# A two-layer vision kernel on one core: V loads one step ahead, score matmuls of two units in one block, and six small changes of order

## The chip, the cores and the metric

The kernel runs on one core of a Trainium2 chip. Times are microseconds on the device, from the start of the program to its end. Engines are named as in the profile: PE is TensorE (the matrix engine; PEld is its loading of weights), DVE is VectorE, ACT is ScalarE, POOL is GpSimd, and SP is SyncE, whose queue issues all the transfers (DMAs) of this kernel in program order. SBUF is the on-chip memory, PSUM the eight banks that PE writes and the other engines read.

## The reference, cut to what matters

The input `x` is 2 images of 56 x 56 tokens with 384 channels, all in float32. Two layers follow each other.

```python
# layer 0
def layer0(x):
    qkv = layer_norm(x) @ w_qkv + b_qkv          # 12 heads of 32; q is scaled by 32 ** -0.5
    # each query sees the 7 x 7 keys around it (the window is moved inside at the borders)
    scores = einsum('bnhwd,bnhwkd->bnhwk', q, k_nb) + bias   # bias by relative position, per head
    attn = softmax(scores)
    x = x + einsum('bnhwk,bnhwkd->bnhwd', attn, v_nb) @ w_proj + b_proj
    return x + gelu(layer_norm(x) @ w1 + b1) @ w2 + b2       # hidden width 1536

# layer 1
def layer1(x):
    p = layer_norm(x) @ w_in + b_in              # inner width 768
    local = depthwise_conv_3x3(p)
    lr, rl = ema(local, axis=W), ema(local, axis=W, reverse=True)    # y = 0.6 * y_before + 0.4 * x
    tb, bt = ema(local, axis=H), ema(local, axis=H, reverse=True)
    mixed = layer_norm(0.25 * (lr + rl + tb + bt) + local)
    x = x + mixed @ w_out + b_out
    return x + gelu(layer_norm(x) @ w1 + b1) @ w2 + b2
```

## The kernel before, in words

The order of the instructions is written out by hand; the framework only adds the waits that data, buffers and banks ask for. Each engine runs its own instructions in program order, so an instruction that waits holds everything behind it on its engine.

**Attention, 0 to about 725 us.** The work is cut into 14 groups (`n`) of 8 image rows, a group into 4 windows (`j`) of 8 x 14 = 112 queries (`TT`), and a window into 3 units (`hg`) of 4 heads each. That makes 56 windows and 168 units. The loop over `s` (L692) has one step for each unit and four more. The keys that a window's queries see are cut into two chunks, in the middle rows and inner columns into three, of 100 to 120 keys (`m` is the number of chunks): 108 units have two chunks and 60 have three. Ahead of the loop stands a startup (L632–676) that normalises the first groups and makes their queries, keys and values.

In step `s`, PE makes the scores of unit `s` (`scores`, L508: per chunk four matmuls, one for each head, on 32 rows of the array each). They are written to two tiles `sc[0]` and `sc[1]`, two heads in each and one bank per head. Then it applies the values of unit `s - 2` (`values`, L544) and sums the numerators with a matrix of ones (L550), and then takes one piece of full-size work, if one is left: queries or keys of a later group (L385), values of a later group (L423), or a projected tile of the output (L569); in some steps also transposes of normalised input (L356). In the same step DVE takes what PE made in the step before (for instance L577, the projected tile plus the residual `xr`), then adds the bias to the scores in two halves (`biased`, L521), then adds up the chunks of unit `s - 1` (`gathered`, L534). ACT makes the exponentials (L528) and evicts the queries, keys and values (L395, L410, L430).

When a window's three units are done, its output is copied (`take`, L477), and its sums of exponentials are transposed (`gather`, L481) and put by POOL into a column of `history` (L482). A step later `invert` makes the reciprocals (L486) and POOL spreads them (`wide`, L488). A step after that `divide` transposes them back (L492) and multiplies (L494). At the end of the stage two operations over `history` and a minimum (L803–809) decide whether all sums were in a safe range; if not, attention is made again by a slow path, which does not run here.

A window's values are loaded from DRAM into a tile `vt` (L464), one transfer for each chunk, when the `Window` object is made, which is in the step of its own first unit; `vt` has two buffers. The other transfers of a step are issued before it, in this order: stores (`store_all`, L629), residuals (`load_residual`, L558, three buffers `xr`, each free when its store has landed), bias tables (L315, 1344 KB), and in the last windows the parts of the MLP's weights (L612, 768 KB each).

**MLP 1 and the way in, about 725 to 1725 us.** The tokens go in groups of up to four tiles of 128 (`groups`). Per group PE makes 12 hidden tiles (`hidden`, L1035; evicted with GELU by ACT, L1044), then the output rows (`tokens`, L1051; added and measured by DVE in the loop at L1379), and the input projection of layer 1 (`project_in`). Beside it, DVE makes the convolution and the running means of layer 1, image by image: `Band` for the 3 x 3 convolution and the scans along rows, `Columns` for the scans along columns. These are cut into small steps, and `beside.go(us)` lets as many of them into the program as fit the given time, at each place where it is called. `Columns` first turns its input around: `turn` (L1171–1180) makes four copies of 128 x 392 on ACT. `turn` is called from three places: from `steps` if nothing was turned before (the first unit of work of each image), again inside the first half, and by the unit of work ahead of it. The result goes to DRAM (`mix_d`).

**The way out and MLP 2, about 1725 us to the end.** Here a group's mixed tiles are loaded (`load_mix`), measured (`measure`, L1238: PE transposes them, DVE takes the statistics), projected (`project_out`, L1252–1261, on PE L1051 with `w_out`, added by DVE at L1258), and the second MLP follows. `measure_beside` (L1244) puts a tile's measurement behind every second hidden tile of the group before; `half_way` is the first group that holds tokens of the second image, whose mixed tiles are the last to be finished.

Layer norms are made by `Norm`: statistics on DVE (L214, L215), `close` (L219 on DVE, then a power on POOL, L222), `shift` (L233), and an application on DVE (`apply`) or ACT (`apply_by_scalar`, L240).

Of the kernel before, what the change touches and what calls it, by code (L numbers as in the profile page):

```python
# [173 lines left out]
def block_kernel(ctx: ExitStack, tc: tile.TileContext, ins: dict, out: bass.AP):  # L174
# [114 lines left out]
    history = lp.tile([P, len(windows), BLOCKS], F32, name="history")  # L289
# [144 lines left out]
    def shift_by_values(pool, psum, wproj, shift):  # L434

        bv = pool.tile([P, NC, P], F32, name="bv")
# [13 lines left out]
    class Window:  # L450
        def __init__(self, i):
# [9 lines left out]
            self.vt = lp.tile([P, 3, C], F32, name="vt", bufs=2)  # L461
# [17 lines left out]
        def gather(self):  # L479
            turned = lp.tile([P, BLOCKS, HD], F32, name="turned")  # L480
            nc.vector.transpose(turned.rearrange("p a b -> p (a b)"), sums[:, : BLOCKS * HD])  # L481
            nc.gpsimd.tensor_copy(history[:, self.i, :], turned[:, :, 0])  # L482

        def invert(self):
            rec = sm.tile([P, BLOCKS], F32, name="rec")
            nc.vector.reciprocal(rec, history[:, self.i, :])  # L486
# [3 lines left out]
        def divide(self):  # L490
            rec = lp.tile([P, BLOCKS * HD], F32, name="rec_t")
# [5 lines left out]
    class Unit:  # L497
# [3 lines left out]
        def scores(self):  # L501

            w, hg = self.w, self.hg
            for c, a in enumerate(w.starts):
                r = w.r0 + a
                for i in range(4):
                    d = slice(i * HD, (i + 1) * HD)
                    nc.tensor.matmul(  # L508
                        sc[i // 2][: w.keys, i % 2, c * TT : (c + 1) * TT],
# [3 lines left out]
            self.pts = lp.tile([P, 4, 3, TT], F32, name="pts", bufs=3)  # L513
# [4 lines left out]
        def biased(self, half):  # L518

            n, h = self.w.keys, 2 * half  # L520
            nc.vector.tensor_tensor(  # L521
                self.of(half),
                sc[half][:n, :, : self.m * TT].rearrange("p h (c q) -> p h c q", q=TT),
# [109 lines left out]
    for h in range(0, NT, 2):  # L633
        norm = Norm(sm)
        for k in range(2):
            norm.add(k, [xgs[0][:, h + k, :]])
        norm.close(2, TT)
        for k in range(2):
            norm.apply(k, xgs[0][:, h + k, :], xgs[0][:, h + k, :])
            for c in range(NC):  # L640
                turn_x(0, h + k, c, tps[c])
# [21 lines left out]
    for t in tiles_of(1)[:2]:  # L663
        value(t, any_bank)()
        store_all()
    for m in range(NC, 2 * NC):
        query_or_key(1, m, any_bank)()
    store_all()
    for k in range(NT):
        normalize_x(2, k)  # L670
# [16 lines left out]
    ng = len(groups_a)  # L687


    END, THEN = ng - 2, (7, 9, 11, 13, 16, 19, 22)  # L690
    for s in range(NU + 4):
# [25 lines left out]
        if s == NU - UG - 4:  # L717
            ectx.close()
            wm = ctx.enter_context(tc.tile_pool(name="w_mlp", bufs=1, side="right"))
            w1, w2, w_parts = weights(0)  # L720
        if s >= NU - UG - 4 and hg == 2 and w_parts:
# [17 lines left out]
        if s < NU:  # L739
            if hg == 0:  # L740
                ws[i] = Window(i)
            units[s] = Unit(ws[i], hg)
            units[s].scores()
# [787 lines left out]
```

## Time and profile before

| | |
|---|---|
| three runs | 2734.52, 2735.04, 2737.29 us; median 2735.04 |
| the profiled execution | 2735.71 us, of which the span from the first instruction to the last is 2733.8 |
| mean granted PE clock | 0.991 |
| busy in the span | PE 2686.1 us (98%), DVE 1663.0 (61%), PEld 1505.5, ACT 907.5, POOL 239.1 |
| attention, 0–725 us | PE 696.4, DVE 513.0, ACT 366.8 |
| MLP 1 and way in, 725–1725 | PE 992.4, DVE 674.0, ACT 324.0 |
| way out and MLP 2, 1725–2733.8 | PE 997.4, DVE 476.0, ACT 216.8 |
| transfers | 298.9 MB, 109 GB/s in the mean |

The profile is of one execution. In the timeline each row begins with the start and the length in microseconds; then come the engine, the line of the kernel (L508 is line 508), the operation, its output and inputs by name with their shapes, the number of equal instructions in a row, and in brackets the idle time of the engine just before it, with what ended it. "PE L544 ... [3.13 <-DMA vt<-v_d]" says that PE stood 3.13 us and went on when the load of `vt` had landed. Rows of SPq are transfers being issued; how long the queue stood before one shows in the distance of the starts. Matmuls run pipelined and their ends are modelled, so a PE that is shown busy may be stretched by a wait or by a lower clock. The distance from one start to the next is the surer measure.

### The profile page before, as it was taken

The page shows a single profiled execution, that of the slowest core. Times are in us where ns is not written, and L with a number is a line of the kernel's source. Part 1 is how long each engine was busy: PE and PEld are TensorE (multiplying, and loading weights), DVE is VectorE, ACT ScalarE, POOL GpSimd, SP SyncE. Part 2 cuts the span into 40 slices and gives each one's busy share as a digit, 9 for nine tenths or more (in the row PEclk, how much of TensorE's full clock was granted, in tenths as well). Part 3 has the DMA queues.
Part 4 walks back from the last instruction along what each step waited for, and adds up shares of the span by engine and source line. Part 5 has one row for each costly group of instructions (what it writes and reads, how often), then busy time and mean ns, then how long its engine had stood idle before and what let it go on. Part 6 is the DMA issues. An engine that isn't in the chain of part 4 may idle for free. (4 is left out here: it accounts for less than half of the span.)

```text
span 2733.8 us, 36207 instructions
## 1 busy us (share of the span) xinstructions
PE 2686.1 (98%) x14975; PEld 1505.5 (55%) x14975; DVE 1663.0 (61%) x2449; ACT 907.5 (33%) x1455; POOL 239.1 (9%) x256
## 2 busy tenths in 40 slices
PE   8999999999899999999999999999999999999998
PEld 4566656665655555555545555455555555555565
DVE  3778767777421188688988889888798422221110
ACT  4555555554322332222344422311233211111111
POOL 0111111110211100000000000000000011110100
PEclk9999999999999999999999999999999999999999
DMA  6322444224411122232355444433454410011000
GB/s 206 131 93 92 155 165 150 76 74 154 155 35 38 63 88 103 86 129 101 120 184 195 180 151 154 163 128 114 147 200 158 151 47 25 28 44 35 29 12 16
DMA packets 131887, 298.91 MB, mean 109 GB/s; under 512 B 10646, under 2 KB 87552, under 8 KB 129408
## 3 DMA queue, kind: packets, MB, share of 16 engines
q1 hardware_dynamic: 131712, 296.50, 31.2%
q8 instruction: 119, 1.95, 0.3%
q14 instruction: 56, 0.46, 0.1%
HBM read 180.86 MB, written 115.61 MB: 108 GB/s over the span
## 5 line engine op out<-in xcount | busy, mean ns | idle before, releaser
L1035 PE MATMUL mm<-hT,w 128*128 128x512 f32 (+2 forms) x1872 | 778.7, 571 | 3.9 <-ACT hid L1044 3.8
L1051 PE MATMUL y<-w,hid 128*128 128x384 f32 x2352 | 764.8, 486 | 0.0
L1051 PEld LDWEIGHTS y<-w,hid 128*128 128x128 f32 x2352 | 445.0, 190 | 305.2 <-issue 0.5
L1035 PEld LDWEIGHTS mm<-hT,w 128*128 128x128 f32 x1872 | 352.5, 191 | 378.1 <-issue 343.1
L1044 ACT ACTIVATE hid<-mm,chan 128x512 f32<-128x512 f32 (+2 forms) x312 | 206.0, 661 | 744.8 <-PE mm L1035 744.7
L1129 DVE SCALAR_TENSOR_TENSOR loc<-pt,taps,loc 128x990 f32<-128x990 f32 (+9 forms) x336 | 377.0, 1122 | 8.3
L521 DVE TENSOR_TENSOR pts<-sc,bias 119x448 f32<-119x448 f32 (+3 forms) x336 | 220.8, 699 | 97.9 <-PE sc L508 97.0
L528 ACT ACTIVATE pts<-pts 119x448 f32<-119x448 f32 (+3 forms) x336 | 206.5, 641 | 194.6 <-DVE pts L521 194.4
L222 POOL TENSOR_TENSOR rs<-rs,mhalf 128x4 f32<-128x4 f32 (+4 forms) x67 | 87.3, 1303 | 1794.5 <-DVE rs L219 1788.0
L385 PE MATMUL ps<-hT,wqkv 128*128 128x448 f32 x504 | 211.5, 558 | 0.6 <-ACT hT L361 0.4
L1051 PE MATMUL y<-w_out,mx 128*128 128x384 f32 x588 | 193.7, 489 | 3.2 <-DVE xc L1258 3.2
L1035 PE MATMUL mm<-hT,w_in 128*128 128x512 f32 (+2 forms) x468 | 191.7, 568 | 0.6 <-ACT hT L254 0.6
L1381 DVE TENSOR_TENSOR xc<-y,xa 128x384 f32<-128x384 f32 x49 | 27.3, 557 | 252.1 <-PE y L1051 251.7
L1432 DVE TENSOR_TENSOR xc<-y,xc 128x384 f32<-128x384 f32 x49 | 27.2, 556 | 219.5 <-PE y L1051 169.2
L1051 PEld LDWEIGHTS y<-w_out,mx 128*128 128x128 f32 x588 | 112.5, 191 | 84.7 <-issue 6.8
L508 PEld LDWEIGHTS sc<-qT,kT 32*100 32x100 f32 (+3 forms) x3168 | 97.8, 171 | 91.3 <-DVE pts L521 17.7
L240 ACT ACTIVATE xn<-xc,sh,rs 128x384 f32<-128x384 f32 x98 | 64.7, 698 | 248.6 <-DVE sh L233 248.4
L1035 PEld LDWEIGHTS mm<-hT,w_in 128*128 128x128 f32 x468 | 88.8, 190 | 101.5 <-issue 91.6
L214 DVE BATCH_NORM_STATS2 st<-xi 128x6 f32<-128x384 f32 x98 | 50.3, 554 | 154.2 <-PE xi L1238 154.1
L508 PE MATMUL sc<-qT,kT 32*100 32x112 f32 (+3 forms) x3168 | 130.9, 279 | 8.6 <-DVE pts L521 7.8
L385 PEld LDWEIGHTS ps<-hT,wqkv 128*128 128x128 f32 x504 | 90.0, 191 | 79.5 <-issue 74.8
L254 ACT ACTIVATE hT<-tp,chan 128x512 f32<-128x512 f32 (+2 forms) x117 | 79.4, 750 | 152.5 <-PE tp L251 152.4
(88 smaller groups left out, 2421.5 us busy)
## 6 DMA issues: line engine op xcount, KB each, us to landing
bias<-in_bias_t SPq DMA_DIRECT2D x16, 1344.0 KB
loc<-loc_d SPq DMA_DIRECT2D x24, 784.0 KB
mixed<-mix_d SPq DMA_DIRECT2D x24, 784.0 KB
mix_d<-mixed SPq DMA_DIRECT2D x24, 784.0 KB
xa<-x_d SPq DMA_DIRECT2D x22, 768.0 KB
p_d<-mx SPq DMA_DIRECT2D x10, 1536.0 KB
mx<-mix_d SPq DMA_DIRECT2D x10, 1536.0 KB
pt<-p_d SPq DMA_DIRECT2D x18, 560.0 KB
```

The lines of the kernel that those rows point to most:

```text
L214: nc.vector.bn_stats(st[:n, i, :], x)
L222: nc.gpsimd.tensor_tensor(rs, rs, mhalf[:n, :k], ALU.pow)
L240: nc.scalar.activation(out[:, k, :], x[:, k, :], AF.Identity, bias=self.sh[:n, k : k + 1], scale=self.rs[:n, k : k + 1],)
L254: nc.scalar.activation(dst[:, c, : len(xs) * n], tp, AF.Identity, bias=col(b, c), scale=col(g, c))
L385: nc.tensor.matmul(ps, lhsT=wqkv[:, c, m * P : (m + 1) * P], rhs=hT[:, c, half_of(n)], start=c == 0, stop=c == NC - 1,)
L508: nc.tensor.matmul(sc[i // 2][: w.keys, i % 2, c * TT : (c + 1) * TT], lhsT=kT[d, hg, w.keys_at + r * w.kc : w.keys_at + (r + w.rows) * w.kc],
L521: nc.vector.tensor_tensor(self.of(half), sc[half][:n, :, : self.m * TT].rearrange("p h (c q) -> p h c q", q=TT), self.w.bias[:n, 4 * self. ...
L528: nc.scalar.activation(self.of(half), self.of(half), AF.Exp)
L1035: nc.tensor.matmul(ps[:, : n * P], lhsT=w[:, c, m * P : (m + 1) * P], rhs=hT[:, c, : n * P], start=c == 0, stop=c == NC - 1,)
L1044: nc.scalar.activation(t[:, : n * P], ps[:, : n * P], AF.Gelu, bias=col(b1, m))
L1051: nc.tensor.matmul(ps, lhsT=t[:, k * P : (k + 1) * P], rhs=w[:, m, :], start=m == 0, stop=m == len(lhs) - 1,)
L1129: nc.vector.scalar_tensor_tensor(to, pt[:, lo + dy - self.top : hi + dy - self.top, xt : xt + n], self.tap(dy, dx), to, ALU.mult, ALU.add,)
```

## The change

Six things are changed.

1. `V` is asked for one step ahead. The next window is made, and so its values are loaded, in the step of the third unit of the window before it, ahead of that step's weight part; `vt` has three buffers instead of two. The first window is made before the loop.
2. If the chunks of unit `s` and of unit `s + 1` fit together into a bank (2 + 2 chunks of 112 are 448 of 512), both units' scores are made in step `s`, the second's behind the first's in the same four banks. Step `s + 1` then begins with the values of unit `s - 1`. This gives 53 pairs. Bias-adds keep their place; the tile `pts` is taken in the first of them.
3. `history` is gone. Each window keeps its own `totals`, and `invert` updates a running flag `good` (128 x 11) with two more DVE operations. Two of the operations at the end of the stage go. To make room, `rec_t` shares the buffer of `turned`, and the `bv` of `shift_by_values` takes a buffer of `vs`.
4. In the startup the statistics of both halves of the first group come before the applications, and group 2 is normalised ahead of group 1's keys instead of behind them.
5. The turn that `steps` makes itself, the first of each image, is on POOL instead of ACT; the other turns stay on ACT.
6. `beside.go(ROW)` is left out behind the last row of the last MLP 1 group, and the measurement of the mixed tiles of group `half_way` comes two hidden tiles later.

```diff
     BLOCKS = -(-NC * TT // HD)
-    history = lp.tile([P, len(windows), BLOCKS], F32, name="history")
+    good = lp.tile([P, BLOCKS], F32, name="good")
+    nc.vector.memset(good, 1.0)
...
-        bv = pool.tile([P, NC, P], F32, name="bv")
+        bv = pool.tile([P, C], F32, name="vs", bufs=2).rearrange("p (c q) -> p c q", c=NC)
...
-            self.vt = lp.tile([P, 3, C], F32, name="vt", bufs=2)
+            self.vt = lp.tile([P, 3, C], F32, name="vt", bufs=3)
...
         def gather(self):
-            turned = lp.tile([P, BLOCKS, HD], F32, name="turned")
+            turned = lp.tile([P, BLOCKS, HD], F32, name="turned", tag="turned")
             nc.vector.transpose(turned.rearrange("p a b -> p (a b)"), sums[:, : BLOCKS * HD])
-            nc.gpsimd.tensor_copy(history[:, self.i, :], turned[:, :, 0])
+            self.totals = sm.tile([P, BLOCKS], F32, name="totals")
+            nc.gpsimd.tensor_copy(self.totals, turned[:, :, 0])
 
         def invert(self):
             rec = sm.tile([P, BLOCKS], F32, name="rec")
-            nc.vector.reciprocal(rec, history[:, self.i, :])
+            nc.vector.reciprocal(rec, self.totals)
+            for edge, inside in ((SUM_MAX, ALU.is_le), (1.0 / SUM_MAX, ALU.is_ge)):
+                nc.vector.scalar_tensor_tensor(good, self.totals, edge, good, inside, ALU.mult)
...
         def divide(self):
-            rec = lp.tile([P, BLOCKS * HD], F32, name="rec_t")
+            rec = lp.tile([P, BLOCKS * HD], F32, name="rec_t", tag="turned")
...
-        def scores(self):
+        def scores(self, first=0):
+            self.first = first * TT
...
-                        sc[i // 2][: w.keys, i % 2, c * TT : (c + 1) * TT],
+                        sc[i // 2][: w.keys, i % 2, (first + c) * TT : (first + c + 1) * TT],
...
-            self.pts = lp.tile([P, 4, 3, TT], F32, name="pts", bufs=3)
...
         def biased(self, half):
+            if half == 0:
+                self.pts = lp.tile([P, 4, 3, TT], F32, name="pts", bufs=3)
+            at = slice(self.first, self.first + self.m * TT)
...
-                sc[half][:n, :, : self.m * TT].rearrange("p h (c q) -> p h c q", q=TT),
+                self.of(half), sc[half][:n, :, at].rearrange("p h (c q) -> p h c q", q=TT),
...
-    for h in range(0, NT, 2):
-        norm = Norm(sm)
+    halves = [Norm(sm) for h in range(2)]
+    for h, norm in enumerate(halves):
         for k in range(2):
-            norm.add(k, [xgs[0][:, h + k, :]])
+            norm.add(k, [xgs[0][:, 2 * h + k, :]])
         norm.close(2, TT)
+    for h, norm in enumerate(halves):
         for k in range(2):
-            norm.apply(k, xgs[0][:, h + k, :], xgs[0][:, h + k, :])
+            x = xgs[0][:, 2 * h + k, :]
+            norm.apply(k, x, x)
             for c in range(NC):
-                turn_x(0, h + k, c, tps[c])
+                turn_x(0, 2 * h + k, c, tps[c])
...
+    for k in range(NT):
+        normalize_x(2, k)
     for m in range(NC, 2 * NC):
         query_or_key(1, m, any_bank)()
     store_all()
-    for k in range(NT):
-        normalize_x(2, k)
...
+    ws[0] = Window(0)
...
+        if s < NU and hg == 2 and s + 1 < NU:
+            ws[i + 1] = Window(i + 1)
         if s >= NU - UG - 4 and hg == 2 and w_parts:
             w_parts.pop(0)()
...
-            if hg == 0:
-                ws[i] = Window(i)
-            units[s] = Unit(ws[i], hg)
-            units[s].scores()
+            if s not in units:
+                units[s] = Unit(ws[i], hg)
+                units[s].scores()
+                behind = Unit(ws[(s + 1) // NC], (s + 1) % NC) if s + 1 < NU else None
+                if behind is not None and (units[s].m + behind.m) * TT <= BANK:
+                    behind.scores(units[s].m)
+                    units[s + 1] = behind
...
-    every = history.rearrange("p w k -> p (w k)")
-    good = lp.tile(every.shape, F32, name="good")
-    nc.vector.tensor_scalar(good, every, SUM_MAX, 1.0, ALU.is_le, ALU.mult)
-    nc.vector.scalar_tensor_tensor(good, every, 1.0 / SUM_MAX, good, ALU.is_ge, ALU.mult)
...
-            def turn(self):
+            def turn(self, copy):
...
-                        nc.scalar.copy(
+                        copy(
...
             def steps(self):
                 if not self.lines:
-                    self.turn()
+                    self.turn(nc.gpsimd.tensor_copy)
...
-                            self.turn()
+                            self.turn(nc.scalar.copy)
...
-                    behind.turn()
+                    behind.turn(nc.scalar.copy)
...
-        def measure_beside(m, g, ahead):
+        def measure_beside(m, g, ahead, late=0):
             n = dgroups[g][1]
-            if m % 2 == 1 and 0 < m // 2 <= n:
-                measure(ahead[0], ahead[2], m // 2 - 1)
-            if m == 10:
+            k = (m - late) // 2 - 1
+            if m % 2 == 1 and 0 <= k < n:
+                measure(ahead[0], ahead[2], k)
+            if m == min(10 + late, NHID - 1):
                 ahead[2].close(n)
...
-                beside.go(ROW)
+                if g < last or k < n - 1:
+                    beside.go(ROW)
...
-                    measure_beside(m, g + 1, ahead)
+                    measure_beside(m, g + 1, ahead, 2 if g + 1 == half_way else 0)
```

More of the change, by code (lines that the diff above doesn't have):

```diff
@@ L520, in biased @@
             n, h = self.w.keys, 2 * half
+            if half == 0:
+                self.pts = lp.tile([P, 4, 3, TT], F32, name="pts", bufs=3)
+            at = slice(self.first, self.first + self.m * TT)
             nc.vector.tensor_tensor(
-                self.of(half),
-                sc[half][:n, :, : self.m * TT].rearrange("p h (c q) -> p h c q", q=TT),
+                self.of(half), sc[half][:n, :, at].rearrange("p h (c q) -> p h c q", q=TT),
                 self.w.bias[:n, 4 * self.hg + h : 4 * self.hg + h + 2], ALU.add,
```

## The prediction

> **What bounds the kernel now.** I read the page's busy shares first: TensorE is the bound nearly everywhere, but its share counts waiting matmuls, whose ends are modelled.
>
> ```profile
> PE 2686.1 (98%) x14975; PEld 1505.5 (55%) x14975; DVE 1663.0 (61%) x2449; ACT 907.5 (33%) x1455; POOL 239.1 (9%) x256
> L521 DVE TENSOR_TENSOR pts<-sc,bias 119x448 f32<-119x448 f32 (+3 forms) x336 | 220.8, 699 | 97.9 <-PE sc L508 97.0
> ```
>
> So a gain must remove matmuls, or gaps before them. None is removed: the matmul count of the sources is equal. I therefore compared, through the whole trace, the distance between the starts of successive matmul groups with that group's usual distance. The excess is about 60 us, nearly all in nine places: 5.4 before 20 us, 8.6 at 43–52, 4.2 at 66–79, 5.5 at 588–602, some 23 at 634–725, 7.1 at 1390–1407, 0.8 at 1492, 5.2 at 1712 and 5.1 at 2160. The stretch view shows the largest; its columns are length, busy time of PE, PEld, DVE, ACT and POOL, clock, DMA share and GB/s:
>
> ```profile
> 588.00:602.00 14.00, 11.75 (x223) 7.74 (x219) 11.90 (x19) 6.80 (x11) 0.68 (x2) 0.88 0.11 34
> 650.50:707.80 57.30, 46.87 (x701) 29.78 (x701) 40.30 (x78) 19.43 (x38) 8.14 (x15) 0.82 0.61 198
> ```
>
> In 650–708 (the last windows of attention) VectorE has 40.3 us of work in 57.3 us, and the clock is 0.82. The timeline there, PE and then the DMA queue:
>
> ```profile
> 682.58 0.78 PE L508 MATMUL sc<-qT,kT 32*120 32x112 f32 x16
> 686.49 0.60 PE L544 MATMUL o<-pts,vt 120*32 120x112 f32 x8 [3.13 <-DMA vt<-v_d]
> 688.07 0.60 PE L544 MATMUL o<-pts,vt 120*32 120x112 f32 x8 [0.98 <-DMA vt<-v_d]
> ```
>
> ```profile
> 672.77 0.42 SPq L629 DMA_DIRECT2D x_d<-xr  x1
> 681.78 0.33 SPq L558 DMA_DIRECT2D xr<-in_x  x1
> 682.21 1.53 SPq L464 DMA_DIRECT2D vt<-v_d  x2
> ```
>
> The residual load L558 sits 9.0 us on the store that frees its buffer, and the V load L464 is queued behind it. Four more places, by the timeline:
>
> ```profile
> 43.82 0.91 ACT L410 ACTIVATE kT<-ps,chan 128x272 f32<-128x272 f32 x2 [1.35 <-PE ps L385]
> 44.62 2.49 ACT L240 ACTIVATE xg<-xg,sh,rs 112x384 f32<-112x384 f32 x4
> 45.38 0.32 PE L356 MATMUL ps<-ident,xg 112*128 112x112 f32 x1 [1.59 <-ACT xg L240]
> 48.20 3.69 PE L441 MATMUL ps<-wproj,bv 128*128 128x384 f32 x6
> ...
> 1394.55 0.92 ACT L1176 COPY line<-loc 128x392 f32<-128x392 f32 x1 [5.10 <-DMA loc<-loc_d]
> 1399.53 1.82 ACT L1044 ACTIVATE hid<-mm,chan 128x512 f32<-128x512 f32 x3
> 1400.26 11.06 PE L1035 MATMUL mm<-hT,w 128*128 128x512 f32 x18 [3.81 <-ACT hid L1044]
> ...
> 1706.33 5.09 DVE L1129 SCALAR_TENSOR_TENSOR loc<-pt,taps,loc 128x990 f32<-128x990 f32 x4
> 1711.45 2.26 DVE L1076 TENSOR_TENSOR_SCAN both<-decay,loc 128x1008 f32<-128x1008 f32 x1
> 1715.98 9.70 PE L1051 MATMUL y<-w_out,mx 128*128 128x384 f32 x24 [3.23 <-DVE xc L1258]
> ...
> 2164.59 1.51 PE L1238 MATMUL xi<-ident,mx 128*128 128x128 f32 x6 [3.47 <-DMA mx<-mix_d]
> ```
>
> In each, PE waits for one engine or transfer whose queue holds something less urgent in front.
>
> **What the Trainium skill says.** "TensorE: Matmul & The Clock Gate", section "What's actually happening": the array falls to half clock after an idle window of about 3.4 us and needs as long of work to rise. The trace agrees in the cost, though the gaps there are only 1.59 and three of 0.28: L441's six matmuls behind them take 3.69 us where warm ones of this shape are worth 1.95. So each stall is priced with its cold tail. "PSUM — Partial Sum Buffer", section "PSUM bank collisions raise a hardware error": accesses are guarded by bank and 32-partition quadrant, not by address; so the first bias-add of a pair has to wait for both units' scores. No stretch of before shows it. "GPSIMD Engine Reference", section 3.1: two-input work is about twice as slow there as on VectorE, and the best rate is near 1.8 cycles an element, an estimate of 0.6 us for 392 elements. The trace's POOL copy of 352 elements takes 0.48 us and agrees. "DMA: Bandwidth & Descriptors", section "Two DMAs through the same engine are not ordered": only a completion orders them, which is why L558 waits for a landing.
>
> **The change, part by part.**
>
> *V one step ahead.* vt(i+1) is issued at the third unit of window i, in front of that step's weight part (768 KB) and of the following residual load. The vt waits in 634–725 are 1.5 (658.0), 3.2 (683.1), 1.4 (686.7), 0.4 and 1.0: 7.5 us, and the half clock behind them costs about 4.5: 12 at most. The floor is VectorE: 40.3 us plus five times the new 0.33 (below) is 42, so 57.3 can't fall under about 43. What is late next: the residual loads at steps 155, 157 and 159 still wait 7.5, 5.0 and 9.0 us for their stores, and two V loads sit behind them; with the steps quicker (2.75 us each at VectorE's pace) these arrive near their need. I leave 4 of the 12: **−8**, ends −4 and −13. In the steady state nothing waits for vt, so nothing is won there.
>
> *Scores in pairs.* 53 pairs of two-chunk units; by the order of instructions 7 lie in the first windows, 7 in the tail, 39 between, and with those of the edges that run full some 42 count. A separate score block costs its turn-in: full work to scores takes 415 ns against 322 within a group, 93 more; its four waves 574 to the values; the values' first wave is 24 above the rest. Removed per pair: 93+574+24 = 691. Added: the 16 matmuls appended to the first block, four waves of 95.5 = 382; and a turn from full work straight into values, never seen before: bounds 0 to 218, taken 176 (93 plus the 83 that the weights' first load costs in full work). Net 558 − 691: −0.13 us a pair. About 14 pairs then have two full pieces close together on one bank; the eviction ends 1.05–1.48 us after the last matmul starts and PE returns in 1.18–1.76, a wait of 0.09. The bias-adds' slack before the next scores is typically 1.9 us (two chunks), and a pair takes 0.58 of it. 42 × 0.13 − 14 × 0.09 = 4.3: **−4.3**; the two bounds of the turn give −10 and about −2, and I keep +4 for waits at the bank.
>
> *History becomes `good`.* Two VectorE operations of 128x11 a window. The nearest rows are 0.16 (L219) and 0.22 (L486): Taken as 0.165 each, 0.33 × 56 = 18 us of VectorE time, hidden in the slack named above, which falls to 0.2 in three-chunk windows; uncovered only at 588–602, where DVE is busy 11.9 of 14, **+0.3**, and in the tail, counted. If none were covered it would cost 18. The end test (0.47 + 0.80 at 723.6–724.9) goes; PE is busy with the MLP's first matmuls soon after: 0.
>
> *Startup.* All statistics first: the last tile of x lands at 6.5 us and must still be measured, and then 12 transposes queue at once instead of six: **0** ± 0.3. `normalize_x(2)` ahead of K(1): ACT gets L240 at about 37.6–40.1 instead of 44.62; sh is ready at 35.24, and four activations of 0.62 delay K's evictions, which have PE's remaining K work as cover. The first scores come at about 46.8 instead of 51.82: **−5.0**, ends −3 and −5.5.
>
> *Steps 0–14.* With pairs, a step there has two Q/K pieces in a row on one bank (+0.9) and values that wait for a take and a bias-add (1.4 and 2.3), while some of the 4.2 us goes: **+1.0**.
>
> *First turn on POOL.* At 1390–1407 ACT stands at L1176 for a landing, L1044 is late behind it and PE loses 3.97 plus six cold matmuls at 0.42, less overlaps: 7.1. On POOL the wait blocks the rs chain alone, whose L222 came at 1393.87, before it, and next 45 us later. Four copies cost 2.1–3.7 us there. **−7.1**, ends 0 and −7.1. The second image's turn at 1970 had 29.6 us of ACT idle and no PE stall: 0.
>
> *No beside work after the last MLP1 row.* L1129 ×4 and L1076 (7.5 us) leave the front of the rs that L1258 and PE wait for at 1712: 3.4 of stall and 1.8 cold, **−5.2**. The work moves on, so its consumers come later: at 2153 the store of mix_d has 8.8 us of VectorE work ahead where it had 3.2, so mx lands near 2170 instead of 2164.4. The measurement moves two hidden tiles later, 2161.0 to 2166.1: stall 4.3 + 1.5 cold against 5.1, **+0.7**, ends −5 and +3.
>
> Sum: −8 −4.3 +0.3 +0 −5.0 +1.0 −7.1 −5.2 +0.7 = −27.6. The profiled run was 2735.71 us around a span of 2733.8, 0.67 above the median 2735.04; so 2735.04 − 27.6 = **2707.4**.
>
> **Rivals.**
> (1) *The stall only moves* (0.22): the residual stores' landings govern the tail (−3), POOL's turn holds part of its stall (−4), the mix stall grows (+3), pairs give 0: −5 −3 −4 −5.2 +3 +1.3 ≈ −13, 2722. For it: the SP queue above; against: the stalls at 43 and 1712 have no second waiter in sight.
> (2) *More than the sum* (0.10): the tail runs at VectorE's floor (−13) and the pairs at −10: 2697. For it: 40.3 of 57.3; against: SP.
> (3) *Slower: the pair makes PE wait* (0.09). The bias-add waits for both units' scores, then full work, take and values follow too tightly, and half clock after it. It outweighs the other 23 us at 23/53 = 0.44 us a pair, and at 0.7 gives +14: 2749. For it: the bank rule and a tail with no full work between; against: 1.9 us of slack.
> (4) *Little change* (0.04): pairs lose 0.4 each (+21) and the rest stands: 2733.
>
> **How the numbers follow.** The sum has 0.55, its own range 2698–2716. With (2) below and (1) above, leaving out (3), (4) and the outer ends, 2695–2722 holds 8 in 10. A difference of 0.2%, 5.5 us, is about what can be told from none. Faster: 0.55 + 0.22 + 0.10 = 0.87; within: 0.04; slower: 0.09.
>
> **What would show it.** Right: scores at about 47 us; no vt wait over 2 us in the tail, whose length is near 49 at a clock over 0.85; L1044 without a wait at 1400; L1258 within 2 us of its rows at about 1690; still one mx wait near 2135. Wrong: values that wait for L528 or L534 in second steps of pairs, scores that wait for L521 in the steady state, rs on POOL late behind the turn, or period from window to window in 130–580 us that isn't shorter.

## The result and the profile after

The changed kernel takes 2709.43 us (median of four runs, 2708.13 to 2711.71) against 2735.57 for the kernel before: a ratio of 0.9903, with an interval of 0.9888 to 0.9919. The forecast was 2707.4. The profiled execution has a span of 2707.7 us, 26.1 less than before. The first lines of its page, to be held against those of before:

```profile
PE 2659.7 (98%) x14975; PEld 1492.9 (55%) x14975; DVE 1679.7 (62%) x2560; ACT 897.7 (33%) x1447; POOL 249.6 (9%) x264
L530 DVE TENSOR_TENSOR pts<-sc,bias 119x448 f32<-119x448 f32 (+3 forms) x336 | 220.8, 699 | 67.7 <-PE sc L515 66.7
```

There are as many matmuls as before, 14975. VectorE has 17 us more to do, and its bias-adds wait 30 us less for scores.

Where the time went is read best from the starts of particular PE instructions, in both traces. Here "unit n" is the start of the sums (L550, after L558) of unit n, "MLP" the first hidden matmul, "rows" the output rows (L1051, after L1063) and "hidden" L1035 (after L1047), by number. Each stretch is the distance from the mark before it, in us:

| stretch | before | after | difference | the prediction's term |
|---|---|---|---|---|
| start to first scores | 51.82 | 48.46 | −3.36 | −5.0 |
| to unit 15 | 63.37 | 61.78 | −1.59 | +1.0 |
| to unit 120 | 419.28 | 413.69 | −5.59 | −4.3, with the tail's pairs |
| to unit 150 | 115.55 | 115.56 | 0.0 | +0.3 |
| to unit 167 | 57.44 | 47.19 | −10.25 | −8 |
| to MLP | 17.69 | 22.84 | +5.15 | none |
| to the first row | 17.89 | 18.87 | +0.98 | none |
| to hidden 900 | 584.92 | 584.92 | 0.0 | 0 |
| to hidden 1100 (first turn) | 158.83 | 151.69 | −7.14 | −7.1 |
| to row 1100 | 193.54 | 193.56 | 0.0 | 0 |
| to row 1400 (last MLP 1 row) | 189.05 | 183.86 | −5.19 | −5.2 |
| to row 1800 | 233.53 | 233.53 | 0.0 | 0 |
| to row 2400 (mixed tiles late) | 338.01 | 339.36 | +1.35 | +0.7 |
| to the last row | 284.57 | 284.57 | 0.0 | 0 |

Four places of the changed kernel by its timeline, which answer to the four of before:

```profile
39.12 2.50 ACT L240 ACTIVATE xg<-xg,sh,rs 112x384 f32<-112x384 f32 x4
45.27 1.31 PE L357 MATMUL ps<-ident,xg 112*128 112x112 f32 x12
46.42 2.11 PE L442 MATMUL ps<-wproj,vs 128*128 128x384 f32 x6
48.46 1.03 PE L515 MATMUL sc<-qT,kT 32*102 32x112 f32 x32
...
1380.94 0.90 POOL L1188 COPY line<-loc 128x392 f32<-128x392 f32 x1
1381.84 0.69 ACT L1056 ACTIVATE hid<-mm,chan 128x512 f32<-128x512 f32 x1 [1.89 <-PE mm L1047]
1382.07 4.11 POOL L1188 COPY line<-loc 128x392 f32<-128x392 f32 x3 [0.23 <-DMA loc<-loc_d]
...
1683.07 15.64 PE L1063 MATMUL y<-w_out,mx 128*128 128x384 f32 x48
1687.15 0.62 DVE L1272 SCALAR_TENSOR_TENSOR xc<-y,rs,xa 128x384 f32<-128x384 f32 x1 [0.93 <-PE y L1063]
...
2144.14 1.51 PE L1251 MATMUL xi<-ident,mx 128*128 128x128 f32 x6 [4.83 <-DMA mx<-mix_d]
```

The twelve transposes run without a gap and the six matmuls of `shift_by_values` warm, 2.11 us instead of 3.69. The evictions go on beside POOL's copies, which wait for the landing in ACT's place. L1272 waits for PE now, where PE waited for it. Only the wait for mx has grown, from 3.47 us to 4.83.

The end of attention needs two rows for each kernel. First before (unit 150 to 167, then to the first row), then the same two stretches of the changed kernel:

```profile
650.02:707.46 57.44, 46.90 (x709) 29.74 (x701) 40.78 (x79) 19.43 (x38) 8.42 (x16) 0.82 0.62 201
707.46:743.04 35.58, 33.34 (x139) 24.64 (x140) 13.78 (x33) 11.97 (x22) 12.45 (x12) 0.95 0.52 172
```

```profile
639.49:686.68 47.19, 36.37 (x709) 23.96 (x701) 41.39 (x89) 19.05 (x38) 8.61 (x16) 1.00 0.64 202
686.68:728.39 41.71, 34.33 (x139) 25.32 (x140) 11.97 (x33) 12.27 (x23) 12.27 (x12) 0.88 0.57 176
```

VectorE's 41.4 us now fill most of the 47.2, and the clock is full. But 6.1 of the 10.3 us won are lost again between the last unit and the MLP's first row. PE's waits in the changed kernel over both stretches say where (line waited at, line waited for, us in total, times, longest):

```profile
PE tp L251 <- DVE bad L820: 7.4, 1, 7.4
PE sc L515 <- DVE pts L530: 5.0, 6, 1.5
PE o L552 <- DMA vt<-v_d: 3.4, 5, 1.0
PE sums L558 <- DVE sum L542: 2.1, 3, 1.2
```

The 7.4 us are not L820's, which takes 0.15. Ahead of it on VectorE stand the last projected tiles, and these stand for residuals (L585 waits 3.23 us for POOL's L571); between them the statistics of the MLP's first tokens stand 3.75 us for `xa`, whose load is issued right behind the last residuals. SP's queue shows why all of these are late:

```profile
672.66 0.44 SPq L637 DMA_DIRECT2D x_d<-xr  x1
679.04 0.33 SPq L566 DMA_DIRECT2D xr<-in_x  x1
679.47 1.50 SPq L465 DMA_DIRECT2D vt<-v_d  x2
681.01 0.46 SPq L620 DMA_DIRECT2D w<-in_L_conv_w  x1
681.58 0.43 SPq L637 DMA_DIRECT2D x_d<-xr  x1
687.50 0.33 SPq L566 DMA_DIRECT2D xr<-in_x  x1
687.88 0.43 SPq L620 DMA_DIRECT2D w<-in_L_conv_w  x1
688.36 0.50 SPq L637 DMA_DIRECT2D x_d<-xr  x1
693.33 2.23 SPq L566 DMA_DIRECT2D xr<-in_x  x5
```

From start to start, each residual load follows the store that frees its buffer by 5 to 6.4 us, and in the trace each goes out 0.02 us or less behind that store's landing. Everything else is issued without a gap between: from end to end the queue either issues or stands on a store. The five last residuals go out at 693.33, and the MLP begins 16.2 us later. In the kernel before it was 16.7 us (708.41 to 725.15).

### The profile page after: what moved, and what is told of

Read it like the earlier page. It is cut to its first block, busy times and chain, and to the rows that moved or that the text cites. A ratio compares the mean times of both kernels' runs of the same rounds, so it can differ in the third digit from the quotient of the medians.

```text
span 2707.7 us, 36333 instructions
## 1 busy us (share of the span) xinstructions
PE 2659.7 (98%) x14975; PEld 1492.9 (55%) x14975; DVE 1679.7 (62%) x2560; ACT 897.7 (33%) x1447; POOL 249.6 (9%) x264
## 5 line engine op out<-in xcount | busy, mean ns | idle before, releaser
L1047 PE MATMUL mm<-hT,w 128*128 128x512 f32 (+2 forms) x1872 | 776.1, 570 | 0.1
L1063 PE MATMUL y<-w,hid 128*128 128x384 f32 x2352 | 764.8, 486 | 0.0
L1063 PEld LDWEIGHTS y<-w,hid 128*128 128x128 f32 x2352 | 445.0, 190 | 305.3 <-issue 0.5
L1047 PEld LDWEIGHTS mm<-hT,w 128*128 128x128 f32 x1872 | 352.1, 191 | 372.8 <-issue 342.4
L386 PE MATMUL ps<-hT,wqkv 128*128 128x448 f32 x504 | 211.9, 559 | 3.5 <-ACT vs L431 1.5
L1047 PE MATMUL mm<-hT,w_in 128*128 128x512 f32 (+2 forms) x468 | 191.7, 568 | 0.6 <-ACT hT L254 0.6
L1063 PE MATMUL y<-w_out,mx 128*128 128x384 f32 x588 | 191.8, 486 | 0.0
L1063 PEld LDWEIGHTS y<-w_out,mx 128*128 128x128 f32 x588 | 111.6, 190 | 79.8 <-issue 4.8
L240 ACT ACTIVATE xn<-xc,sh,rs 128x384 f32<-128x384 f32 x98 | 64.7, 698 | 269.3 <-DVE sh L233 269.1
L1047 PEld LDWEIGHTS mm<-hT,w_in 128*128 128x128 f32 x468 | 88.7, 190 | 101.6 <-issue 91.8
L386 PEld LDWEIGHTS ps<-hT,wqkv 128*128 128x128 f32 x504 | 90.2, 191 | 84.4 <-issue 72.8
L515 PEld LDWEIGHTS sc<-qT,kT 32*100 32x100 f32 (+3 forms) x3168 | 90.9, 169 | 69.5 <-DVE pts L530 17.3
L515 PE MATMUL sc<-qT,kT 32*100 32x112 f32 (+3 forms) x3168 | 113.8, 270 | 9.0 <-DVE pts L530 8.4
```

Source lines behind the costliest of these rows:

```text
L240: nc.scalar.activation(out[:, k, :], x[:, k, :], AF.Identity, bias=self.sh[:n, k : k + 1], scale=self.rs[:n, k : k + 1],)
L386: nc.tensor.matmul(ps, lhsT=wqkv[:, c, m * P : (m + 1) * P], rhs=hT[:, c, half_of(n)], start=c == 0, stop=c == NC - 1,)
L515: nc.tensor.matmul(sc[i // 2][: w.keys, i % 2, (first + c) * TT : (first + c + 1) * TT], lhsT=kT[d, hg, w.keys_at + r * w.kc : w.keys_at + ...
L1047: nc.tensor.matmul(ps[:, : n * P], lhsT=w[:, c, m * P : (m + 1) * P], rhs=hT[:, c, : n * P], start=c == 0, stop=c == NC - 1,)
L1063: nc.tensor.matmul(ps, lhsT=t[:, k * P : (k + 1) * P], rhs=w[:, m, :], start=m == 0, stop=m == len(lhs) - 1,)
```

## The experiments

All of them are edits of the changed kernel, but for one; their stretches are in one table behind them. "Tail" below is unit 150 to the MLP. The times of five of them (the row kept, three parts undone, the sums twice, no pairs with V late, and the kernel before again) are of one execution each.

**Without pairs.**

```diff
-                if behind is not None and (units[s].m + behind.m) * TT <= BANK:
+                if False and behind is not None and (units[s].m + behind.m) * TT <= BANK:
```

> The changed kernel with the scores of each unit made in its own step. In the changed kernel unit 15 to unit 150 (start of the sums) takes 529.2 us, before 534.8; unit 150 to the MLP's first matmul 70.0, before 75.1; the first scores to unit 15 61.8, before 63.4. Theory: a pair saves about 0.14 us of TensorE time and nothing else, and the tail is set by V and by the residual stores on SP's queue. Then unit 15 to 150 takes 534.5 to 535, the tail 70 plus or minus 1.5, the start about 63, the whole 2715 to 2718. Rival: the gain between 15 and 150 is not the pairs' (529 stays). Second rival: the pairs win the tail, as VectorE waits less for scores: then the tail takes 74 to 76.

Measured: 2718.71 us, ratio to before 0.9929 (0.9912 to 0.9945). Unit 15 to 120 takes 419.28 again, to the hundredth as before: the whole 5.6 us are the pairs', and the new operations on the sums cost nothing there. The steps to unit 15 stay at 61.68, so the 1.6 us won in them are not the pairs'. The tail takes 74.5, which was the second rival's number, so the theory was wrong there; the whole is 0.7 us over its range.

**V where it was.** The window object is made early, its transfers are issued in its own first step.

```diff
             self.vt = lp.tile([P, 3, C], F32, name="vt", bufs=3)
+        def fetch(self):
             for c, a in enumerate(self.starts):
...
+            if hg == 0:
+                ws[i].fetch()
```

> The changed kernel, pairs and three buffers kept, with the V transfers issued where they were before: in the step of the window's own first unit, behind that step's residual load and the weight part of the step before. Theory of the prediction: nothing moves between unit 15 and 150 (529.2 us), and the tail from unit 150 to the MLP's first matmul goes from 70.0 to 75 to 79, with PE waits on vt of 5 us and more; the whole 2714 to 2718. Rival: the stores of the residual govern the tail wherever V stands, then 70 to 71.5 and the whole within 2 us of 2709.4. Second rival: in a pair that spans two windows the late V delays the steady state too, then unit 15 to 150 takes over 531.

Measured: 2710.9 us, ratio 0.9905 (0.9888 to 0.9921). My theory is wrong and the first rival right within 0.1 us: the tail takes 71.6. PE does wait for V, as its waits in unit 150 to the first row show:

```profile
PE o L554 <- DMA vt<-v_d: 9.5, 5, 6.0
PE sc L517 <- DVE pts L532: 3.5, 5, 1.5
PE tp L251 <- DVE bad L823: 0.8, 1, 0.8
```

It waits 6.1 us more for V than in the changed kernel, and 6.6 less at L251. A wait that the trace names was not what set the time.

**Weights behind.** Each weight part one step later, behind that step's residual.

```diff
-        if s >= NU - UG - 4 and hg == 2 and w_parts:
+        if NU - UG - 4 < s < NU and hg == 0 and w_parts:
             w_parts.pop(0)()
...
             xs = {g: load_group(x1f, groups[g], "xa") for g in range(2)}
+            while w_parts:
+                w_parts.pop(0)()
```

> The changed kernel with each of the first five weight parts of 768 KB issued one step later, behind that step's store and residual load, and the sixth behind the loads of the MLP's first tokens. Theory: what is late in the tail of the changed kernel is SP's chain of a store, its landing (5 to 9 us, behind a weight part and a bias table), the residual load, and V behind it. With the weights out of the way a landing takes 2 to 4 us, the tail from unit 150 to the MLP's first matmul falls from 70.0 to 61 to 66, and the whole to 2701 to 2706. Rival: VectorE's work (39 us of 57) sets the pace, then the tail stays at 69 to 70. Second rival: the weights come too late for the MLP, which shows as waits of its matmuls on w and takes the gain back.

Measured: 2707.43 us, ratio 0.9891 (0.9872 to 0.9909), the tail 68.9: far from the theory's 61 to 66 and just under the first rival's 69 to 70. The residual loads still stand 4.7 to 7.2 us on their stores. The parts are still being moved when the next store is issued: one issued at 668.75 lands by 675.06, and the store issued behind it at 670.83 lands by 676.40. So the place of the parts in the queue explains at most a small share, but this run did not take them out of the stores' way, and what their bytes cost stays open.

**The row kept**, and **three parts undone** at far-off places:

```diff
-                if g < last or k < n - 1:
-                    beside.go(ROW)
+                beside.go(ROW)
```

> The changed kernel with the beside work behind the last row of the last MLP 1 group put back; the measurement two tiles later is kept. Theory: the stall at the first projected tile of the way out returns (5.2 us), but VectorE's work is then done earlier, so that the store of the mixed tiles comes about 5.5 us earlier against the hidden tiles of the group that measures them, and the wait of 4.8 us on mx with 1.5 us of slow matmuls behind it goes: in sum 0 to 1.5 us faster than the changed kernel, 2708 to 2709.5. Rival: the transfers themselves set the landing of mx, then the wait stays and the whole is 5 us slower, 2714 to 2715.

> The changed kernel with three parts undone, each of another stretch: the first turn back on ACT, the measurement of the mixed tiles not later, and the normalisation of group 2 back behind group 1's keys. By the prediction's terms: the hidden tiles at 1376 to 1407 lose 7.1 us; the wait for mx near 2140 grows by the 5.15 us of two hidden tiles; the first scores come at 50.5 to 52 instead of 47.4 to 48.5. Whole 2725 to 2728. Rival for the turn: its transfer lands earlier in the new order, then it costs 0 to 3. Rival for the measurement: mx lands as PE asks for it, then 0 to 2.

The second puts `nc.scalar.copy` back into the first turn, passes no `late`, and moves `normalize_x(2, k)` back behind group 1's keys. Measured: 2711.08 and 2726.28 us. The second is in its range; the first is 1.6 us over its own.

The turn gives back what it had won: hidden 900 to 1100 takes 159.02, 7.3 us more, with the old pattern.

```profile
1384.48 0.92 ACT L1188 COPY line<-loc 128x392 f32<-128x392 f32 x1 [5.48 <-DMA loc<-loc_d]
1390.15 10.91 PE L1047 MATMUL mm<-hT,w 128*128 128x512 f32 x18 [4.14 <-ACT hid L1056]
```

The first scores come at 51.77, against 46.5 to 48.5 in all kernels that normalise group 2 early. The row and the later measurement make a square together. From row 1100 to row 2400 it takes 760.6 and 762.2 us with neither (before, profiled twice), 762.7 with the row left out alone, 756.8 with the later measurement alone, and 756.8 with both. So what the missing row wins at the first place (5.2 to 6.5 us) it loses at the second: VectorE's 7.5 us only move. With the row kept the sum of both places is the changed kernel's to 0.1 us; what the whole is longer lies elsewhere. With the row kept, the store of the mixed tiles is issued 3.1 us into the group that measures them, and PE doesn't wait:

```profile
2131.28 15.61 PE L1047 MATMUL mm<-hT,w 128*128 128x512 f32 x36
2134.41 1.11 SPq L1226 DMA_DIRECT2D mix_d<-mixed  x2
2146.73 0.82 PE L1251 MATMUL xi<-ident,mx 128*128 128x128 f32 x6
```

With it left out and the measurement not moved, the store comes 8.5 us into it, and PE waits twice as long:

```profile
2135.28 10.46 PE L1047 MATMUL mm<-hT,w 128*128 128x512 f32 x24
2143.82 1.11 SPq L1226 DMA_DIRECT2D mix_d<-mixed  x2
2155.42 1.51 PE L1251 MATMUL xi<-ident,mx 128*128 128x128 f32 x6 [9.68 <-DMA mx<-mix_d]
```

**Twice the work on the sums**, and the startup's statistics in the old order:

```diff
-                nc.vector.scalar_tensor_tensor(good, self.totals, edge, good, inside, ALU.mult)
+                for again in range(2):
+                    nc.vector.scalar_tensor_tensor(good, self.totals, edge, good, inside, ALU.mult)
```

> The changed kernel with the two new VectorE operations on the sums made twice over (18 us more of VectorE time in all; the output is the same), and with the startup's statistics and applications in the old order. Theory: hidden in the steady state, unit 15 to 120 stays at 413.7 within 0.4; uncovered in the three-chunk steps without full work, where unit 120 to 150 grows from 115.5 by 1.5 to 2.5, and in the tail by 0 to 2. The first query or key matmul comes at 10.7 to 11.1 instead of 10.0 to 10.25. Whole 2711 to 2715. Rival: small operations stretch every step, by up to 18 us in all.

Measured: 2717.18 us, over the upper end. Unit 15 to 120 grows by 2.1 us, which I had excluded, and unit 120 to 150 by 2.6. The first query or key matmul comes at 11.44, against 9.84 to 10.82 with the new order; but the first scores come at 47.98, inside the range of the others, so that gain is gone again by then. The steps to unit 15 take 63.3 again.

**Residuals two steps later**, so that the store before has landed when SP comes to the load. Theory: the queue is the tail's bound, and V's early place only lets it wait for something else. (`loaded` counts the steps until POOL adds to a residual; 2 instead of 4 keeps that addition in its old step.)

```diff
-                load.append(t + 3)
+                load.append([t + 3, 2])
...
-        while load:
-            load_residual(load.pop(0))
+        for one in list(load):
+            if one[1] == 0 or s >= NU:
+                load.remove(one)
+                load_residual(one[0])
+                loaded[one[0]] = 2
+            one[1] -= 1
```

> The changed kernel with each residual load issued two steps later, when the store that frees its buffer has had time to land, so that SP's queue is not held by it. In the changed kernel and in the run with the row kept, which has the same attention, the residual loads of the tail are issued at the same times within 0.7 us though PE's progress differs by 3 us. Theory: SP's chain of store, landing (5 to 9 us), load, V and weights, one turn of it for each of six projected tiles, sets the tail, and it is the blocked queue, not the weights' bytes. Then vt waits vanish, and unit 150 to the MLP's first matmul falls from 70.0 and 71.9 to 60 to 66; the whole 2699 to 2705. Rival: VectorE's 41.4 us of work and its waits for PE's projected tiles set the pace; then the tail stays at 68 to 72. Second rival: the residuals come too late, which shows as VectorE waiting for xr, and the tail is longer than 72.

Measured: 2705.69 us, ratio 0.9891 (0.9874 to 0.9907). The vt waits vanish, and the tail is 67.6, between the theory's 60 to 66 and the rival's 68 to 72; the whole is 0.7 us over the theory's range. To the first row it is 84.5 against 88.9 to 91.1. Unit 15 to 120 loses 2.3 us, though. By the whole alone this run can't be told from the changed kernel: the intervals overlap.

**Both mended.** The same with the mixed tiles measured behind the last four hidden tiles:

```diff
-            k = (m - late) // 2 - 1
-            if m % 2 == 1 and 0 <= k < n:
+            k = m - NHID + 4 if late else m // 2 - 1
+            if (late or m % 2 == 1) and 0 <= k < n:
```

> The residual loads two steps later, as above, and the four measurements of the mixed tiles of the group half way put behind the last four hidden tiles, one behind each, instead of every second from the sixth. Theory: they start 7.7 us later, so the 4.8 us of waiting for mx and the 1.5 of slow matmuls behind it go, 5 to 6.5 us in all between the output rows 1800 and 2400 (339.4 in the changed kernel), and what closes the norm stays ahead of its use. Whole 2693 to 2700, faster than both kernels. Rival: packed transposes wait for VectorE's statistics and the norm comes late, then 0 to 3 of it are left.

Measured: 2698.41 us, ratio 0.9871 (0.9850 to 0.9893). Rows 1800 to 2400 take 332.87, 6.5 less, and the tail 63.8. The attention is that of the run before, where the tail was 67.6: that is how far it scatters.

**Two corners more.** Without pairs and with V late; the kernel before once again; and the last version with the later residuals from step 144 on only (`tail = END * UG <= s < NU`, otherwise at once as before).

> The changed kernel without pairs and with V where it was: the fourth corner beside the changed kernel (unit 150 to the first output row 88.9), no pairs (92.9) and V late (88.6). Theory after those: V's place moves nothing by itself, so this takes 92 to 94, as without pairs, and the whole is 2716 to 2720. Rival: V one step ahead is what the tail needs once the pairs are gone, then 96 or more and the whole over 2721.

> The kernel before, profiled once more, for the scatter of the stretches: if unit 150 to the first output row takes 91 to 95 (93.0 in the first profile), the gain of the tail in the changed kernel (88.9, 91.1 and 89.6 in three profiles of the same attention) is outside the scatter; if it takes 89 to 91, it isn't. Unit 15 to 120 should take 419.3 again within 0.2, and the first scores to unit 15 63.4 within 0.3, or else the 1.6 us gained there are scatter.

> As the run with the later residual loads and the packed measurements, but with the later loads from step 144 on only. In the two runs with them the stretch from unit 15 to 120 took 415.9 to 416.2 instead of 413.7, so they cost over 2 us in the steady state. Theory: this comes back (413.5 to 414), unit 150 to the first output row stays at 80 to 85 against 88.9 to 91.1, and the packed measurements keep their 6.5 us: the whole 2693 to 2699. Rival: the tail's 80.7 was chance and it takes 87 or more, then 2700 to 2704.

Measured: 2715.49, 2741.14 and 2698.95 us, the last with a ratio of 0.9872 (0.9855 to 0.9888) and inside its range. The first two missed: without pairs and with V late, unit 150 to the first row takes 90.6, under the 92 to 94 of the theory and far from the rival's 96, and the whole is 0.5 us under its range. The kernel before again takes 91.3 there, as said, and 63.4 to unit 15; but its first scores come 3 us later than in its first profile, and unit 15 to 120 takes 1.2 us more where I had allowed 0.2. The two kernels without pairs have 419.3 and 419.4 there, so the pairs' 5.6 us stand. All the profiles side by side, in us:

| kernel | first scores | to unit 15 | to 120 | to 150 | to 167 | to MLP | to first row | tail |
|---|---|---|---|---|---|---|---|---|
| before | 51.8 | 63.4 | 419.3 | 115.5 | 57.4 | 17.7 | 17.9 | 75.1 |
| before again | 54.8 | 63.4 | 420.5 | 117.1 | 58.3 | 16.0 | 16.9 | 74.4 |
| changed | 48.5 | 61.8 | 413.7 | 115.6 | 47.2 | 22.8 | 18.9 | 70.0 |
| row kept | 47.4 | 61.8 | 413.7 | 115.5 | 51.5 | 20.4 | 19.2 | 71.9 |
| three undone | 51.8 | 61.8 | 413.9 | 115.6 | 50.0 | 21.6 | 17.9 | 71.6 |
| sums twice | 48.0 | 63.3 | 415.8 | 118.2 | 53.9 | 18.9 | 16.9 | 72.9 |
| no pairs | 47.9 | 61.7 | 419.3 | 117.3 | 52.6 | 21.9 | 18.3 | 74.5 |
| no pairs, V late | 46.5 | 61.7 | 419.4 | 115.9 | 57.2 | 16.5 | 16.9 | 73.7 |
| V late | 47.7 | 61.8 | 413.7 | 115.6 | 55.6 | 16.0 | 16.9 | 71.6 |
| weights behind | 47.6 | 61.8 | 413.7 | 115.5 | 51.4 | 17.5 | 18.6 | 68.9 |
| residuals later | 47.1 | 61.8 | 416.0 | 115.6 | 51.6 | 16.0 | 16.9 | 67.6 |
| residuals later, packed | 48.4 | 61.8 | 416.2 | 117.0 | 47.2 | 16.6 | 16.9 | 63.8 |
| later in the tail only, packed | 46.7 | 61.8 | 413.7 | 117.2 | 47.2 | 17.6 | 16.9 | 64.7 |

The three profiles of the same attention and queue order (changed, row kept, three undone) have tails of 70.0, 71.9 and 71.6; the four without pairs have 73.7 to 75.1, whether V is early or late. So the pairs may be worth some 3 us in the tail; but to the first row the ranges overlap (88.6 to 91.1 with pairs and V early or late, 90.6 to 93.0 without), so this is not shown. V's place is worth nothing outside the scatter. With the later residuals the tail is 63.8 to 67.6, and to the first row it is 80.7 to 84.5, clear of all others. The queue shows it best: from unit 150 to the issue of the five last residuals it takes 53.8 to 54.8 us in the three profiles named above, and 48.4 to 49.9 with the later residuals. The last kernel keeps the steady state's 413.7, as its theory said. Its two stretches and PE's waits in them:

```profile
639.37:686.52 47.15, 36.31 (x708) 24.21 (x700) 41.37 (x89) 19.31 (x38) 8.61 (x16) 1.00 0.70 226
686.52:721.05 34.53, 33.49 (x139) 23.98 (x140) 12.98 (x33) 11.99 (x22) 12.41 (x12) 0.95 0.54 179
```

```profile
PE sc L515 <- DVE pts L530: 5.9, 7, 1.5
PE sums L558 <- DVE sum L542: 4.6, 5, 1.2
PE tp L251 <- DVE bad L826: 0.8, 1, 0.8
```

No wait for V is left and 0.8 of the 7.4 us at L251; what PE waits for is VectorE. Against the changed kernel it wins 7.2 us from unit 150 to the first row and 6.5 behind it; 1.6 of this is lost between units 120 and 150, a stretch that varies by as much among kernels that are alike in it (115.5 and 117.1 in the kernel before). The two packed versions were not timed against the changed kernel side by side; against the kernel before, the last one's interval touches the changed kernel's at 0.9888.

## Why the prediction was right, and where its steps were not

The total is right within 2 us, and so is each of its terms but the tail and the first steps. That the total came so close is in part luck: the tail fell 3.9 us short of its term and the startup 1.6, while steps 0 to 14 gave 2.6 more than was forecast and the pairs 1.3. (The nine stalls that the prediction lists add to 65 us, not to about 60; its sum doesn't rest on that.)

- *First turn on POOL*: −7.14 for −7.1, and +7.3 when undone. The parts that the prediction names, 3.97 us and six times 0.42, make only 6.5; the 7.1 was the excess that it had read off the stretch. The estimate of 0.6 us a copy, from the best rate in the Trainium skill's "GPSIMD Engine Reference", section 3.1, was low, and the trace doesn't agree with it: the four copies took 5.0 us (3.5 on ACT) and the first 0.90. It cost nothing, since nothing on POOL was due.
- *No beside work after the last row*: −5.19 for −5.2; and its price at the mixed tiles +1.35 for +0.7, with the store issued 8.6 us into the group, near the 8.8 us of work that were counted ahead of it. The wait is 4.83 us; the prediction took 4.3 where its own times (2170 less 2166.1) make 3.9. What I didn't draw from my own numbers: what the row wins, it loses at the mixed tiles, and the later measurement alone would have been as good.
- *Startup*: −3.4 for −5.0, between −3.4 and −5.3 in the ten profiles with the early normalisation, against the first profile of before; against its second, where the first scores come at 54.8, each is 3 us more. In the changed kernel the wait went ahead: the landing of group 1's input came at 18.1 us instead of 15.7, and V's evictions stood behind L240. The statistics' order (0) wins about 1 us at the first matmul and none at the first scores.
- *Pairs*: −5.6 from unit 15 to 120 alone, where 32 pairs lie, 0.17 us each for 0.13. The term of the sum that was too large is the turn from full work straight into values: it is 469 ns after L386 and 416 after L577, the same as into scores, so 93 more than within a group and not 176. (Its bound of −10 was small too: with a turn of 0 its own figures make −11.7.) A pair's first bias-add waits for both units' scores, as "PSUM — Partial Sum Buffer", section "PSUM bank collisions raise a hardware error", made me expect: it begins at 349.84 us in one pair, 0.3 us behind the start of the last of the 32 matmuls (348.70 to 349.54), and between units 15 and 120 it is never sooner than 0.29 us behind it. Whether the bank asks for this wait, or the framework only sets it because both units share a tile, the traces don't tell. No pair of steps became longer by it: against the run without pairs the two steps of a pair together take 0.19 us less. The wait for a single bank's eviction was there too, some 277 ns for 189 on 8 of the 53 turns from sums to L386 in this stretch.
- *Sums' check*: 0 in the steady state, as said. But the cover is thinner than I had it: twice the work costs 2.1 us there and 2.6 behind it.
- *Steps 0 to 14*: −1.6 for +1.0. It isn't the pairs, nor V's place, nor that of the normalisation; of the edits of the changed kernel, only the one with the old startup order and the doubled sums has the old 63.3. Which of these two it was stays open.

The step that failed is *V one step ahead*, −8. It took the waits on vt for the cause, with their half clock behind them. By the profile PE's waits on vt in the tail fell only from 6.1 us to 3.4. It named what would be late next, the residual loads held by their stores, but left it 4 of 12 us and ended its sum at the last unit. To the last unit it even came true (−10.3), and with it the signs that it had named for being right: no vt wait over 1.0 us, a length near 49 (47.2) and a full clock. But they all lie ahead of the last unit, and behind it 6.1 us came back. The runs put SP's queue in its place: V late costs nothing outside the scatter, later residuals win 2 to 8 us of tail, and the MLP starts 15.2 to 17.6 us after the five last residuals are issued in all profiles but one (19.4, sums twice). So rival (1)'s mechanism held in the tail, with −4.1 to the first row where it had said −3 (−2.4 against the second profile of before).

## What to carry to other kernels

A wait in the trace names the last thing to arrive, which need not be what sets the pace. Follow it to the queue that issued the transfer, look what stands at the queue's head, and carry the count to where the stretch hands over, not to where the wait ends. A load into a buffer that a store has just been asked to free holds everything behind it on that queue: ask for it some steps later, as here, or, which was not tried, have a buffer more. And beside work that is left out at one place comes up at another; look for the next transfer that depends on it before counting the gain.

## What the hardware showed that I had not expected

- The two small VectorE operations on the sums (128x11) take 0.107 us in the mean where POOL does nothing (45 of 112) and 0.318 where it is at work (67), up to 0.92 beside L571's additions. "GPSIMD Engine Reference" of the Trainium skill, section 1, says that POOL shares its SBUF interfaces with VectorE and meets operations with two SBUF inputs, which these have; the trace agrees. In the run with the doubled sums the mean in 118 to 600 us rose from 0.250 to 0.350, so that the doubling cost more than double.
- From the first row to hidden 900 every one of the thirteen profiles takes 584.92 us, while the tail of the same instructions differs by up to 3.8 us (67.6 and 63.8 with the residuals later). The granted clock goes with it: unit 150 to 167 was granted 1.00 in the changed kernel, in 47.2 us, and 0.90 with the row kept, in 51.5, though the attention is the same. Which of the two brings the other about isn't shown:

```profile
638.35:689.84 51.49, 41.26 (x708) 27.18 (x701) 41.44 (x89) 19.42 (x38) 8.61 (x16) 0.90 0.62 196
```

- In the tail of the changed kernel a residual load is issued 3.5 to 9.1 us after the store of 192 KB that frees its buffer, 5.9 in the mean of six. With the weight parts of 768 KB issued behind the loads the mean is still 5.7.
